# Taking the pairs of a gather and scatter loop two at a time

## The chip, the cores and the metric

The kernel runs on one core of a Trainium2 chip. A core has five engines with queues of their own: TensorE (PE, with its weight loads as PEld), VectorE (DVE), ScalarE (ACT), GpSimd (POOL) and SyncE (SP, which here only issues DMAs). The metric is the time of one execution on the device in microseconds, the median of several runs. A profile is one more execution, recorded by the hardware profiler.

## The reference

All is float32. `x` has 12,500 rows of 256. `src`, `dst` and `edge_weight` describe 200,000 edges, sorted by `dst`.

```python
# graph part
z   = layernorm(x)
s   = z @ W
x   = x + segment_sum(s[src] * edge_weight[:, None], dst) + b
# feed-forward part: the mean over all rows picks 2 of 8 experts for all rows
z   = layernorm(x)
w   = routing(mean(z) @ Wr + br)              # softmaxes, top 2, their weights
y_e = gelu(z @ W1[e] + b1[e]) @ W2[e] + b2[e]
x   = x + layernorm(sum_e w_e * y_e + z) * gamma + beta
```

The kernel moves the product with `W` behind the sum: it sums the weighted rows of `z` by `dst` first and multiplies the sums by `W`.

## The kernel before, in words

**Layout.** `acc` (in SBUF) holds the sums of all nodes, transposed: 128 features on the partitions, two halves, one column a node. `xn` (in DRAM) holds the normalised rows. Edges are taken from the highest `dst` down in chunks of 128; four chunks are a super, two supers (8 chunks, 1,024 edges) are a *pair*. There are 180 pairs; the 128 chunks with the lowest `dst`, where edges are dense, are left to the dense path below.

**A pair** has these steps. `gather_pair` (line 480): GpSimd issues eight indirect DMAs (line 486), each of which fetches 128 rows of `xn` into the tile `g`. `select` (437): VectorE builds, for each chunk, a 128x32 matrix with an edge's weight in the column of its node (line 448; in the early pairs lines 462 and 468), and for each super a 128x128 matrix that shifts the four 32-node windows to their places (lines 456 or 472). `multiply` (494), the first sum: TensorE multiplies each chunk's gathered rows by its selection into 32 partitions of the bank `pt` (line 507); a tiny product ahead of it (502) takes the wait for all eight gathers; ACT copies `pt` to `part` (510). `spread_out` (515), the second level: TensorE multiplies `part` by the shifts into the bank `ps` (522), and VectorE adds it to `acc` (541) at a column read from the data. `g` and the selections have three buffers each, `part` two, `pt` and `ps` one bank each.

**The loop over pairs** (898) writes an order by hand, and each engine runs its own instructions in that order: multiply pair i; select and gather pair i+1; spread out pair i-1; the dense steps; jobs; stages. So a gather may start when the multiply of the pair three before has released its buffer.

**Dense path** (`dense_steps`, 683). In the first 44 pairs VectorE builds 128 chunks' one-hot factors (606, 609), TensorE multiplies them (620) and VectorE adds the products to a count matrix kept in a free part of `acc` (634). Then the matrix is multiplied with all rows of `xn` (662), placed, and its room cleared (677). `prepare_dense` (557) makes the keys, from an iota on GpSimd (561), in tiles of its own.

**Stages.** When all edges of a block of 256 nodes are in, four stages follow, one an iteration: `product` (722) multiplies by `W` (730), adds the row and the bias (726, 731) and takes statistics on VectorE; `normalised` (741); `transposed` (754, line 759; the last bias is added at 768); `keep` stores the block's `zT` to DRAM and `enqueue` (879) makes its jobs known. There are 49 blocks. After 24 and after 38 blocks `name_slot` guesses an expert from the mean so far and loads its weights.

**Jobs.** A job is a block under one guessed expert, 98 in all: four first-level steps (`first`, 822, then GELU on ACT, 823) and two second-level ones (`second`, 830, in the one bank `po`, then VectorE's sums, 836). `work(budget)` runs steps as far as a budget goes: PAIR_US - OWN_US - SLACK_US = 6.5 a pair, less 1.9 and 1.3 where stages run. Steps that are left run in the tail, which mixes the experts' outputs by the true weights, normalises them and stores (lines 1022 to 1074). If a guess was wrong or an edge fell outside its window, a slow path recomputes all; with these inputs it isn't taken.

**Banks.** All eight PSUM banks are in use: `bias_ps` (both biases, broadcast once and read from there by lines 726 and 768), `gz`, `ph` twice, `po`, `pt`, `ps`, `dps`.

Of the kernel before, what the change touches and what calls it, by code (L numbers as in the profile page):

```python
# [18 lines left out]
P = 128  # L19
# [88 lines left out]
def gnn_ffn_kernel(  # L108
# [154 lines left out]
    jobs_stack, stack = ExitStack(), ExitStack()  # L263
    with tc.tile_pool(name="rt", bufs=1) as rt, tc.tile_pool(
        name="bias_ps", bufs=1, space=bass.MemoryType.PSUM
    ) as biasp, jobs_stack, stack, tc.manual_schedule():

# [19 lines left out]
        far = rt.tile([P, 2 * NSEG + 2], FP, name="far")  # L287
        apart = rt.tile([1, NSEG], FP, name="apart")

        sumc = rt.tile([P, H, NBLK], FP, name="sumc")  # L290

        bias_ps = biasp.tile([P, 2, D], FP, name="bias_ps")
        with tc.tile_pool(name="once", bufs=1) as once:
            bias_row = once.tile([1, 2, D], FP, name="bias_row")
            nc.scalar.dma_start(bias_row[:, 0], b_gnn[None, :])
            nc.scalar.dma_start(bias_row[:, 1], beta[None, :])
            nc.tensor.matmul(
                bias_ps.rearrange("p k d -> p (k d)"), row, bias_row.rearrange("p k d -> p (k d)"), start=True, stop=True
            )
        edgep = open_pool(name="edges", bufs=2)  # L300
# [13 lines left out]
        def prepare_segment(k):  # L314
# [50 lines left out]
            nc.vector.scalar_tensor_tensor(gap, gap, float(WIN - NARROW), gap, op0=ALU.subtract, op1=ALU.mult)  # L365
            nc.vector.reduce_max(apart[:, k : k + 1], gap, axis=AX.X)
            t.update(base_i=base_i, rel=rel, slot=slot)

# [46 lines left out]

        gp = open_pool(name="gat", bufs=3)
        selp = open_pool(name="sel", bufs=3)
        partp = open_pool(name="part", bufs=2)
        xp = open_pool(name="xrows", bufs=2)
        pps, aps, dps = psum("part_ps", 1), psum("agg_ps", 1), psum("dense_ps", 1)  # L420
        dp = open_pool(name="dense", bufs=1)

# [10 lines left out]
        selections = {}  # L433
        first_load = -(-DENSE_CHUNKS // DENSE_STEP) + 2
        dense_pairs = first_load + -(-(-(-NQ // 4)) // ROWS_STEP) + 1

# [113 lines left out]
        lots = [(c, LOW) for c in range(0, LOW_END, LOW)] + [(c, HIGH) for c in range(LOW_END, DENSE_CHUNKS, HIGH)]  # L550
        wide = dp.tile([P, QW], FP, name="wide")
        place_of = dp.tile([P, DENSE_CHUNKS], FP, name="place_of")
        key = dp.tile([P, DENSE_CHUNKS], FP, name="key")
        dense_w = dp.tile([P, DENSE_CHUNKS], FP, name="dense_w")
        lot_i = dp.tile([1, len(lots)], I32, name="lot_i")

        def prepare_dense():
            C = DENSE_CHUNKS
            with tc.tile_pool(name="dense_once", bufs=1) as op:
                wide_i = op.tile([P, QW], I32, name="wide_i")  # L560
                nc.gpsimd.iota(wide_i, pattern=[[1, QW]], base=0, channel_multiplier=0)
                nc.vector.tensor_copy(wide, wide_i)
                src_i = op.tile([P, C], I32, name="src_d")
                nc.sync.dma_start(src_i, src[:, :C])
                dst_i = op.tile([P, C], I32, name="dst_d")
                nc.sync.dma_start(dst_i, dst[:, :C])
                nc.sync.dma_start(dense_w, edge_weight[:, :C])
                t_i = op.tile([P, C], I32, name="t_i")
                rel = op.tile([P, C], FP, name="rel_d")
                nc.vector.tensor_scalar(t_i, src_i, P - 1, None, ALU.bitwise_and)  # L570
                nc.vector.tensor_copy(place_of, t_i)
                nc.vector.tensor_scalar(src_i, src_i, 7, None, ALU.logical_shift_right)
                nc.vector.tensor_copy(key, src_i)
                nc.vector.tensor_copy(rel, dst_i)

                base = op.tile([1, C], FP, name="base_d")
                for c0, c1, k in ((0, LOW_END, LOW), (LOW_END, C, HIGH)):
                    n = (c1 - c0) // k
                    nc.vector.tensor_scalar(
                        base[:, c0:c1].rearrange("p (g k) -> p g k", k=k),  # L580
                        rel[0:1, c0:c1].rearrange("p (g k) -> p g k", k=k)[:, :, 0:1].to_broadcast([1, n, k]),
                        0.0,
                        float(DENSE - DENSE_WIN),
                        ALU.max,
                        ALU.min,
                    )
                    g0 = c0 // LOW
                    nc.vector.tensor_copy(
                        lot_i[:, g0 : g0 + n], base[:, c0:c1].rearrange("p (g k) -> p g k", k=k)[:, :, 0]
                    )  # L590
                bcast = scratch_ps()[:, :C]
                nc.tensor.matmul(bcast, row, base, start=True, stop=True)
                nc.vector.tensor_tensor(rel, rel, bcast, ALU.subtract)
                nc.vector.scalar_tensor_tensor(key, key, float(DENSE_WIN), rel, op0=ALU.mult, op1=ALU.add)

                nc.vector.scalar_tensor_tensor(rel, rel, DENSE_WIN - 1.0, rel, op0=ALU.subtract, op1=ALU.mult)
                nc.vector.memset(far[:, 2 * NSEG : 2 * NSEG + 1], -1.0)
                nc.vector.reduce_max(far[:, 2 * NSEG + 1 : 2 * NSEG + 2], rel, axis=AX.X)

# [122 lines left out]
        def product(b):  # L722

            t0 = b * TPB
            xt = rows_of.pop(b)
            nc.vector.tensor_tensor(xt, xt, bias_ps[:, 0].unsqueeze(1).to_broadcast([P, TPB, D]), ALU.add)
            ps = gps.tile([P, TPB, D], FP, name="gz")
# [26 lines left out]
        def transposed(b, z):  # L754

            ps = gps.tile([P, H, TB], FP, name="gz")
            for j in range(TPB):
                for h in range(H):
                    nc.tensor.transpose(ps[:, h, j * P : (j + 1) * P], z[:, j, h * P : (h + 1) * P], ident)
            zT = tp.tile([P, H, TB], FP, name="zT")  # L760
            m = min(TB, N - b * TB)
            for h in range(H):
                nc.scalar.activation(zT[:, h, :m], ps[:, h, :m], AF.Copy, accum_out=sumc[:, h, b : b + 1])
                if m < TB:
                    nc.scalar.activation(zT[:, h, m:], ps[:, h, m:], AF.Copy)
            at = nodes(b * TPB, TPB)
            last_bias = halves(bias_ps[:, 1]).unsqueeze(1).to_broadcast([P, TPB, H, P])
            nc.vector.tensor_tensor(at, at, last_bias, ALU.add)
            return zT
# [124 lines left out]
        stage_z = stage_t = stage_k = None  # L894
        select(0)
        before = None
        g = gather_pair(0)
        for i, (s0, n) in enumerate(pairs):
            k, at = seg_of(s0)
            since = 0 if at + n == segs[k][1] else since + 1  # L900
            if k + 1 < NSEG:
                if since == 0 and k > 0:
                    load_segment(k + 1)
                if since == 4:
                    prepare_segment(k + 1)
            part = multiply(i, g)
            if i + 1 < len(pairs):
                select(i + 1)
                g = gather_pair(i + 1)
            if before:  # L910
                spread_out(*before)
            dense_steps(i)
            before = (i, part)
            complete = nxt > 0 and i > 0 and pairs[i - 1][0] <= done_at[nxt]
            budget = min(budget, 0.0) + PAIR_US - OWN_US - SLACK_US
            budget -= 1.9 * complete + 1.3 * (stage_t is not None)
            if i + 1 < len(pairs):
                budget = work(budget)
            if stage_k is not None:
# [6 lines left out]
            if stage_z is not None:  # L926
                stage_t = (stage_z[0], normalised(*stage_z))
                stage_z = None
            if complete:
                stage_z = (nxt, product(nxt))  # L930
                if nxt >= 2:
                    load_rows(nxt - 2)
                nxt -= 1
        spread_out(*before)
        assert nxt == 0 and stage_z is None and stage_t is None and stage_k is None and named == SLOTS
# [5 lines left out]
        vs = open_pool(name="tail_s", bufs=6)  # L941
        mps = psum("mix_ps", 3)
        gam = tailp.tile([P, D], FP, name="gam")
# [65 lines left out]
        def banks():  # L1009
# [4 lines left out]
            while True:  # L1014
                yield from (m, z, m, lambda: bias_ps, m) if jobs_left() else (m, h, z, m, h, lambda: bias_ps, m, o)

# [316 lines left out]
```

## Time and profile before

| | |
|---|---|
| median of 3 runs | 2438.74 us (2431.86 to 2442.75) |
| the profiled execution | 2448.85 us, of which the span of instructions is 2446.9 us |
| TensorE busy | 1718.6 us (70%) |
| GpSimd busy | 1488.0 us (61%), of it gathers 1368.3 us, 1,436 of 953 ns |
| VectorE busy | 1190.5 us (49%) |
| ACT busy | 475.8 us (19%) |
| DMA | 349.17 MB, mean 143 GB/s |
| mean granted TensorE clock | 0.876 |
| first gather starts, last copy of a first sum starts | 87.56 us, 2265.4 us into the span |

A profile's line names the source line, the engine, the operation and the tiles by the program's names, output first. In rows in order of time the first two numbers are start and length in us; what is in brackets is how long the engine had been idle and what, by the semaphores, ended the wait ("issue": nothing that the profile shows; "remote": a source it can't name). Ends of matmuls are modelled by the profiler, not observed.

### The profile page before, as it was taken

What the parts mean: (1) busy time and instruction counts of PE and PEld (TensorE: products, weight loads), DVE (VectorE), ACT (ScalarE), POOL (GpSimd) and SP (SyncE); (2) the same over time, 40 slices, a digit from 0 to 9 for tenths busy, and PEclk for the clock granted to TensorE, in tenths of its full rate; (3) what the DMA queues carried; (4) which work ended last, traced back from release to release, by engine and by line L of the source; (5) the groups of instructions that cost most, each with busy time, mean ns of one, the idle gap of its engine ahead of it and who ended that gap; (6) DMA issues with size and microseconds to landing.
All of it is one profiled execution on the core that took longest, in us unless ns stands there. A gap on an engine that the chain in (4) does not pass through costs nothing.

```text
span 2446.9 us, 29786 instructions
## 1 busy us (share of the span) xinstructions
PE 1718.6 (70%) x9698; PEld 1215.8 (50%) x9698; DVE 1190.5 (49%) x4265; ACT 475.8 (19%) x1085; POOL 1488.0 (61%) x1537
## 2 busy tenths in 40 slices
PE   0056655666567468888888878888887888888775
PEld 0033333333344246656656656566565665565675
DVE  7355555655533544545444444434433433343688
ACT  5201101111101122212122112212121211211233
POOL 5666656665565666666666666666666666665144
PEclk9987767877788779999999989999998999989898
DMA  8533333332375344444444454444444444444486
GB/s 304 193 91 116 103 93 102 109 114 83 116 225 167 110 145 142 136 138 139 141 131 135 138 151 144 133 134 141 133 136 125 137 137 134 130 123 120 160 281 219
DMA packets 167602, 349.17 MB, mean 143 GB/s; under 512 B 33514, under 2 KB 77072, under 8 KB 167440
## 3 DMA queue, kind: packets, MB, share of 16 engines
q0 software_dynamic: 68928, 188.31, 27.2%
q1 hardware_dynamic: 94120, 145.65, 17.6%
q10 hardware_dynamic: 4392, 13.21, 1.4%
q8 instruction: 82, 1.34, 0.2%
q14 instruction: 80, 0.66, 0.1%
HBM read 282.91 MB, written 64.14 MB: 142 GB/s over the span
## 4 chain that ended last, share of the span: by engine, by line
PE 48%; another core or an unknown queue 17%; DVE 16%; issue 12%; ACT 4%; DMA 2%; POOL 1%; SPq 0%; ACTq 0%; DVEq 0%; POOLq 0%
PE ph L822 14%; PE po L830 12%; PE ps L522 5%; PE pt L507 5%; PE dps L620 4%; PE gz L730 3%; DVE st L69 2%; PE dps L662 2%; DVE acc L541 1%; ACT hT L823 1%; ACT xt L393 1%; ACT part L510 1%; DVE nmt L1052 1%; DVE w L609 1%
## 5 line engine op out<-in xcount | busy, mean ns | idle before, releaser
L486 POOL DMA_INDIRECT g<-xn,src_i x1436 | 1368.3, 953 | 810.4 <-issue 394.2
L822 PE MATMUL ph<-zTj,w 128*128 128x256 f32 x1568 | 452.0, 420 | 127.5 <-issue 55.0
L830 PE MATMUL po<-hT,w 128*128 128x256 f32 x1568 | 438.3, 412 | 105.9 <-issue 80.9
L541 DVE TENSOR_TENSOR acc<-acc,ps 128x256 f32 x359 | 151.0, 421 | 678.8 <-remote 293.2
L822 PEld LDWEIGHTS ph<-zTj,w 128*128 128x128 f32 x1568 | 309.9, 208 | 229.0 <-issue 101.7
L830 PEld LDWEIGHTS po<-hT,w 128*128 128x128 f32 x1568 | 314.8, 206 | 197.6 <-issue 125.7
L510 ACT ACTIVATE part<-pt 128x512 f32<-128x512 f32 (+1 forms) x180 | 107.2, 596 | 1145.2 <-remote 596.2
L620 PE MATMUL dps<-w 128*128 128x490 f32 x256 | 151.5, 718 | 146.3 <-DVE acc L634 113.7
L823 ACT ACTIVATE hT<-ph,b 128x256 f32<-128x256 f32 x392 | 178.6, 472 | 311.2 <-PE ph L822 173.2
L448 DVE TENSOR_SCALAR sel<-iota,rel,wgt 128x32 f32<-128x32 f32 x992 | 233.4, 319 | 0.0
L522 PEld LDWEIGHTS ps<-spread,part 128*128 128x128 f32 x1436 | 186.8, 203 | 93.6 <-issue 87.0
L522 PE MATMUL ps<-spread,part 128*128 128x128 f32 x1436 | 223.3, 301 | 11.4 <-DVE acc L541 8.8
L507 PE MATMUL pt<-g,sel 128*32 128x256 f32 x2872 | 219.9, 418 | 0.0
L836 DVE SCALAR_TENSOR_TENSOR yT<-po,b,zTj 128x256 f32<-128x256 f32 x196 | 85.7, 479 | 163.1 <-PE po L830 73.5
L730 PE MATMUL gz<-wg,acc 128*128 128x256 f32 x392 | 120.0, 460 | 49.0 <-remote 15.2
L620 PEld LDWEIGHTS dps<-w 128*128 128x128 f32 x256 | 52.5, 232 | 203.6 <-DVE acc L634 133.8
L502 PE MATMUL pt<-g,sel 128*32 128x8 f32 (+1 forms) x360 | 42.4, 190 | 131.3 <-DMA g<-xn,src_i 71.6
L502 PEld LDWEIGHTS pt<-g,sel 128*32 128x32 f32 x360 | 26.2, 113 | 204.1 <-issue 165.2
L730 PEld LDWEIGHTS gz<-wg,acc 128*128 128x128 f32 x392 | 89.3, 233 | 74.3 <-issue 37.1
L731 DVE TENSOR_TENSOR acc<-gz,xt 128x512 f32<-128x512 f32 x49 | 33.9, 691 | 167.7 <-PE gz L730 107.1
L507 PEld LDWEIGHTS pt<-g,sel 128*32 128x32 f32 x2872 | 98.7, 118 | 26.2 <-issue 8.8
L1044 POOL TENSOR_TENSOR rst<-vet,half 128x4 f32<-128x4 f32 (+1 forms) x25 | 42.4, 1697 | 108.4 <-DVE vet L1042 108.4
(183 smaller groups left out, 1586.6 us busy)
## 6 DMA issues: line engine op xcount, KB each, us to landing
zTj<-zts SPq DMA_DIRECT2D x98, 256.0 KB
yts<-yT SPq DMA_DIRECT2D x98, 256.0 KB
ab<-yts SPq DMA_DIRECT2D x48, 512.0 KB
g<-xn,src_i POOLq DMA_INDIRECT x1436
zts<-zT SPq DMA_DIRECT2D x49, 256.0 KB
xt<-in_x SPq DMA_DIRECT2D x24, 512.0 KB
xn<-xt ACTq DMA_DIRECT2D x24, 512.0 KB
xt<-in_x SPq DMA_DIRECT2D x48, 256.0 KB
```

Of the source, the lines that this page charges most:

```text
L448: nc.vector.tensor_scalar(sel[:, j * SUPER + c], iota[:, :NARROW], t["rel"][:, col], t["wgt"][:, col], ALU.is_equal, ALU.mult,)
L486: nc.gpsimd.indirect_dma_start(out=g[:, j], out_offset=None, in_=xn, in_offset=bass.IndirectOffsetOnAxis(ap=segment[k]["src_i"][:, col : c ...
L507: nc.tensor.matmul(pt[q, j // SUPER], sel[:, j], g[:, j], start=True, stop=True, tile_position=(0, j % SUPER * NARROW))
L510: nc.scalar.activation(part[:, :n], pt[:, :n], AF.Copy)
L522: nc.tensor.matmul(ps[:, j, h], part[:, j, h * P : (h + 1) * P], spread[:, j], start=True, stop=True)
L541: nc.vector.tensor_tensor(at, at, ps[:, j], ALU.add)
L620: nc.tensor.matmul(ps, r, q, start=(c == c0), stop=(c == c0 + k - 1))
L730: nc.tensor.matmul(ps[:, j], node_tile(t0 + j)[:, h], wg[:, h], start=(h == 0), stop=(h == H - 1))
L822: nc.tensor.matmul(ph, w1[:, k, h, c * P : (c + 1) * P], zT[:, h], start=(h == 0), stop=(h == H - 1))
L823: nc.scalar.activation(hT[:, c], ph, AF.Gelu, bias=b1[:, k, c : c + 1])
L830: nc.tensor.matmul(po[:, h], w2[:, k, c, h * P : (h + 1) * P], hT[:, c], start=(c == 0), stop=(c == FC - 1))
L836: nc.vector.scalar_tensor_tensor(yT[:, i], po[:, i], b2[:, k, i : i + 1], zT[:, i], op0=ALU.add, op1=ALU.add)
```

## The change

The loop takes two pairs an iteration, and `g` and the selections get four buffers. Within an iteration the order is now: segment preparation; gather both pairs of the next iteration; a quarter of the jobs; spread out the first pair of the iteration before and its dense steps; a quarter of the jobs; the second pair likewise; select both pairs of the next iteration; the stages with the third quarter; the product of a completed block and the last quarter; then multiply both pairs of this iteration, into two `pt` banks. The budget is twice the old one, and a block's stages advance once an iteration.

The second `pt` bank is `bias_ps`'s: the biases are broadcast through a `ph` bank at the start, copied to SBUF, and read there. The tail's own rotation of banks gets a fourth `mix` bank in its place. The tiles of the dense preparation move into buffers of the job tiles (`hT`, `zTj`), which are not yet in use then. A check is added to the segment preparation (`low_chunk`): that a pair spread while the dense matrix still stands in `acc` doesn't reach into it.

```diff
-    with tc.tile_pool(name="rt", bufs=1) as rt, tc.tile_pool(
-        name="bias_ps", bufs=1, space=bass.MemoryType.PSUM
-    ) as biasp, jobs_stack, stack, tc.manual_schedule():
+    with tc.tile_pool(name="rt", bufs=1) as rt, jobs_stack, stack, tc.manual_schedule():
...
-        apart = rt.tile([1, NSEG], FP, name="apart")
+        apart = rt.tile([1, 2 * NSEG], FP, name="apart")
...
+        low_chunk = SUPER * pairs[dense_pairs + 3][0]
...
-        bias_ps = biasp.tile([P, 2, D], FP, name="bias_ps")
+        bias = rt.tile([P, 2, D], FP, name="bias")
...
+            bias_ps = scratch_ps()
+            nc.tensor.matmul(bias_ps, row, bias_row.rearrange("p k d -> p (k d)"), start=True, stop=True)
+            nc.scalar.activation(bias.rearrange("p k d -> p (k d)"), bias_ps, AF.Copy)
...
+            lo, hi = max(0, low_chunk - s0 * SUPER), min(m, pad)
+            if lo < hi:
+                nc.vector.tensor_scalar(gap[:, lo:hi], base[:, lo:hi], -1.0, float(QH * DENSE), ALU.mult, ALU.add)
+                nc.vector.reduce_max(apart[:, NSEG + k : NSEG + k + 1], gap[:, lo:hi], axis=AX.X)
+            else:
+                nc.vector.memset(apart[:, NSEG + k : NSEG + k + 1], -1.0)
...
-        gp = open_pool(name="gat", bufs=3)
-        selp = open_pool(name="sel", bufs=3)
+        gp = open_pool(name="gat", bufs=4)
+        selp = open_pool(name="sel", bufs=4)
...
-        pps, aps, dps = psum("part_ps", 1), psum("agg_ps", 1), psum("dense_ps", 1)
+        pps, aps, dps = psum("part_ps", 2), psum("agg_ps", 1), psum("dense_ps", 1)
...
+        held = hp.tile([P, FC, TB], FP, name="hT").rearrange("p c t -> p (c t)")
+        wide = held[:, :QW]
...
-            nc.vector.tensor_tensor(xt, xt, bias_ps[:, 0].unsqueeze(1).to_broadcast([P, TPB, D]), ALU.add)
+            nc.vector.tensor_tensor(xt, xt, bias[:, 0].unsqueeze(1).to_broadcast([P, TPB, D]), ALU.add)
...
-        select(0)
-        before = None
-        g = gather_pair(0)
-        for i, (s0, n) in enumerate(pairs):
...
-            part = multiply(i, g)
-            if i + 1 < len(pairs):
-                select(i + 1)
-                g = gather_pair(i + 1)
-            if before:
-                spread_out(*before)
-            dense_steps(i)
-            before = (i, part)
+        def gather_two(i):
+            return [gather_pair(p) for p in range(i, min(i + 2, len(pairs)))]
+
+        for p in range(min(2, len(pairs))):
+            select(p)
+        before = []
+        g = gather_two(0)
+        for i in range(0, len(pairs), 2):
+            two = range(i, min(i + 2, len(pairs)))
+            for p in two:
...
+            ahead = gather_two(i + 2)
             complete = nxt > 0 and i > 0 and pairs[i - 1][0] <= done_at[nxt]
-            budget = min(budget, 0.0) + PAIR_US - OWN_US - SLACK_US
+            budget = min(budget, 0.0) + 2 * (PAIR_US - OWN_US - SLACK_US)
             budget -= 1.9 * complete + 1.3 * (stage_t is not None)
-            if i + 1 < len(pairs):
-                budget = work(budget)
+            part_of = budget / 4
+
+            def some(share):
+
+                nonlocal budget
+                if i + 2 < len(pairs):
+                    budget = share * part_of + work(budget - share * part_of)
+
+            some(3)
+            for b, p in zip(before, two):
+                spread_out(*b)
+                dense_steps(p)
+                some(2)
+            if not before:
+                for p in two:
+                    dense_steps(p)
+            for p in range(i + 2, min(i + 4, len(pairs))):
+                select(p)
             if stage_k is not None:
...
+            some(1)
             if complete:
...
+            some(0)
+            before = [(p, multiply(p, t)) for p, t in zip(two, g)]
+            g = ahead
+        for b in before:
+            spread_out(*b)
...
-        mps = psum("mix_ps", 3)
+        mps = psum("mix_ps", 4)
...
-                yield from (m, z, m, lambda: bias_ps, m) if jobs_left() else (m, h, z, m, h, lambda: bias_ps, m, o)
+                yield from (m, z, m, m, m) if jobs_left() else (m, h, z, m, h, m, m, o)
```

## The prediction

> **What bounds the kernel now.** I read the stages first, then GpSimd's waits, then one pair in order of time. The stages, in microseconds from the span's start (each engine's busy time, then its instructions):
>
> ```profile
> core 0: us, PE busy (x) PEld busy (x) DVE busy (x) ACT busy (x) POOL busy (x), PEclk, DMA share, GB/s
> 174.00:680.00 506.00, 301.07 (x1496) 165.21 (x1496) 291.47 (x932) 58.89 (x152) 310.54 (x320) 0.77 0.36 107
> 680.00:787.00 107.00, 78.37 (x432) 54.97 (x432) 32.15 (x112) 10.84 (x27) 60.92 (x64) 0.86 0.62 194
> 880.00:2260.00 1380.00, 1136.88 (x6409) 834.08 (x6410) 582.39 (x2288) 281.29 (x652) 878.12 (x928) 0.92 0.46 137
> 2260.00:2447.00 187.00, 129.13 (x932) 118.25 (x930) 145.29 (x376) 57.93 (x120) 70.19 (x37) 0.87 0.64 217
> ```
>
> In the long stage 880 to 2260 TensorE is busy 82% and GpSimd 64%, so TensorE looks like the bound. GpSimd's own waits between 900 and 2200 say otherwise (total, times, longest):
>
> ```profile
> POOL g L486 <- issue: 233.0, 763, 0.6
> POOL g L486 <- remote: 132.5, 62, 2.3
> POOL g L486 <- PE ph L822: 76.7, 36, 2.3
> POOL g L486 <- PE po L830: 19.1, 9, 2.2
> ```
>
> 763 waits of 0.30 us lie between two gathers of a pair; some 107 waits (62 + 36 + 9) are all about 2.1 us, one a pair. A late TensorE would leave waits of all lengths. In order of time (start, length, engine; lines left out):
>
> ```profile
> 1401.95 0.60 ACT L510 ACTIVATE part<-pt 128x512 f32<-128x512 f32 x1 [3.25 <-PE po L830]
> 1402.13 0.94 POOL L486 DMA_INDIRECT g<-xn,src_i  x1 [2.16 <-PE po L830]
> ...
> 1407.44 1.03 PE L507 MATMUL pt<-g,sel 128*32 128x256 f32 x13
> ...
> 1408.40 1.16 PE L522 MATMUL ps<-spread,part 128*128 128x128 f32 x8
> ...
> 1410.87 0.95 POOL L486 DMA_INDIRECT g<-xn,src_i  x1 [0.30 <-issue]
> ...
> 1413.81 0.60 ACT L510 ACTIVATE part<-pt 128x512 f32<-128x512 f32 x1 [10.29 <-remote]
> ...
> 1413.99 0.96 POOL L486 DMA_INDIRECT g<-xn,src_i  x1 [2.17 <-remote]
> ...
> 1414.83 1.99 PE L822 MATMUL ph<-zTj,w 128*128 128x256 f32 x8 [0.72 <-ACT hT L823]
> ```
>
> The multiply (L507) starts at 1407.4 and its record ends at 1408.47, but the copy that needs only it (L510) starts at 1413.81, and GpSimd, which needs the multiply's buffer for its next pair, at 1413.99. The last gather had ended at 1411.82. I took this distance for every pair: in 106 of the 115 pairs from number 62 to 176 the copy starts 1.8 to 2.15 us after the last gather's end (median 1.94), while the multiply's record ended a median 6.1 us before the copy. So a multiply issued while gathers run **counts as done only when the gathers have drained**. The loop is closed: eight gathers of 1.25 us less the last 0.30 (9.7), 1.95 of draining, 0.17 of restart = 11.8 us; measured 11.90 a pair there. Whatever follows the multiply is held too: with the semaphore updates in the trace matched to the records, first-level steps (L822) behind a multiply in a burst complete a median 2.92 us after their recorded end (172 of them), those with no multiply ahead of them 0.17 (138).
>
> **Two pairs an iteration.** Call R the release, when both multiplies count as done. GpSimd then gathers 16 without a stop: 16 x 1.25 - 0.30 = 19.7; restart 0.2, draining 1.95: **21.85 us for two pairs** against 2 x 11.90 = 23.8, if TensorE has issued both multiplies by then. Two pauses of 2.1 become one. With four buffers GpSimd never waits inside the 16: the first needs the first multiply, the ninth the second, released together.
>
> Is TensorE there in time? Its passes between 892 and 2211, at their full-clock distance (0.2155 us for 256 columns, 0.11 for 128), make 8.14 us a pair, so 16.3 for two, 14.2 of it ahead of the multiplies (about 1.03 each). At the clock of 0.92 that is 15.5. After a release TensorE resumes 0.7 to 1.9 us late (above 0.72, on ACT's gelu); I take 1.5, with two copies of 0.60 now ahead on ACT. I add 1 for waits on DVE and ACT: R + 18. Then VectorE: selections of both pairs come together, 2 x (8 x 0.319 + 2 x 0.28) = 6.2 us in one piece, and behind them on its queue wait the second level's sums (L836), for which the one po bank and so the next L830 waits. Two first-level steps (1.7) cover part; up to 4 us could be bare, I take 2 in half of the iterations: R + 18 to R + 20, released at the drain or, when just late, some 2 us after. So **22.4**, bounds 21.85 and 23.5.
>
> [...] A multiply is 18 passes with 18 loads; two make 72. [...]
>
> [...]
>
> **The dense stages.** In 174 to 680 a pair takes 12.7 us; TensorE has 5.3 of full-clock work, at 0.77: 13.8 for two. The chain in an iteration: copy 0.8, first spread 1.2, three dense products 3.2 (0.82 each, clock in), the lot's sum 0.9, second spread 1.2, VectorE makes and three products again 4.2, transposes and product 2.8: R + 14.3 to R + 17 with multiplies, under 19.9. Every eighth iteration also prepares a segment in front (L320 to L366, about 5 us). **22.5**. In 680 to 787 the rows' products (24 passes, 6.9 us a pair) make two pairs 15.7/0.86 = 18.3 plus waits: 23.5. Pairs 54 to 63 have little for TensorE: 22.0.
>
> **Start.** Pairs 0 to 3 are gathered in one run (28 gathers, 87.6 to 122.5). The iota of the dense preparation now stands behind 28 gathers on GpSimd's queue instead of 12. It used to run at 102.5; at 122.5, VectorE's cast, the preparation behind it, TensorE's broadcast and both first multiplies wait for it. They can't release their buffers before the drain at 124.5 in any case: R for pairs 0 and 1 is 127.5. The old restart there was 126.7.
>
> **Small edits.** Bias from SBUF: 98 sums of 0.679; by L1068 (128x1024 from SBUF, 1.274, half of it 0.64) 0.64 to 0.68 each, 0 to -4 us of VectorE, hidden since it is busy 42%. The extra check: two small operations in some of 12 segments (L323's 0.21 and L366's 0.27), at most 6 us, same cover; bare they would cost those 6. One more ACT copy at setup, under 1. Gathers, loads and stores keep their number; SP's queue keeps the order of its loads and stores, with those of two pairs together, and the three loads of the dense preparation stay ahead of the first steps. The stage steps advance once in two pairs: by the loop's conditions slots are named at pairs 64 and 112 instead of 61 and 108, and six first and five second steps more stay for the tail (14 and 9 against 8 and 4): 6 x 0.86 + 5 x 1.72 = 13.8 us of TensorE, which has 58 idle there; I take +3 (0 to 14). The tail's banks stay as many.
>
> **The sum.** Start 127.5. Releases of pairs 2 to 177 are 88: 22 x 22.5 + 4 x 23.5 + 5 x 22.0 + 57 x 22.4 = 1976. Loading weights at two namings 5. The last pairs' spreads and multiplies 7.5 (now 2260.4 to 2267). Tail 180 + 3. Together 2299, against the span of 2446.9: 148 less. The profiled execution took 2448.85, span and 2 around it, 10 over the median of 2438.74; the same 10 off 2301 gives **2290**.
>
> **Rivals.** (a) The floor: TensorE is always in time, every step 21.85: 88 x 21.85 = 1923 and 323 for the rest, 2246 span, **2238**. For it: 4.6 us of TensorE's idle a pair are in the hold. (b) TensorE or VectorE often late, still faster: 23.3 a step, **2365**. For it: VectorE's 6.2 us block. (c) No change in the pace: the hold is TensorE's own lateness, or the job steps lose elsewhere what the pause gives: **2440**. Against it: the equal distances. (d) Slower: the multiplies stand last in the order, so every delay of TensorE's queue, above all L830 waiting for L836 behind the selections, goes straight into GpSimd's pause. It decides from a mean step of 24.1 ((2446.9 - 323)/88), which is issue at R + 22; at 25, **2515**. For it: nothing gathers ahead beyond two pairs. Against it: between release and multiply TensorE runs gapless after its resumption, with the clock's share as work.
>
> **Numbers.** Likeliest 0.58 (its own range 2250 to 2345), floor 0.11, (b) 0.16, (c) 0.04, (d) 0.11. The first three are faster: 0.85; same 0.04, slower 0.11. 0.5% is what a measurement here can tell from no change. The range takes in the floor and most of (b): 2230 to 2385.
>
> **What would show it.** GpSimd's pauses half as many, each about 2.1 to 2.7 us, bursts of 16; the copies L510 in couples 1.95 us after a burst's last gather; first-level steps soon done inside a burst; GpSimd busy about 68% in the job stage (16 x 0.95 in 22.4). Wrong would be: pauses over 4 us as a rule (TensorE late; look for L830 <- L836), or steps without a multiply ahead held as well.

## The result, and the profile after

The changed kernel took **2891.2 us** (median of 4 runs, 2879.1 to 2898.0) against 2440.7 before on the same chip (2431.9 to 2449.1): a ratio of **1.187, 95% interval 1.181 to 1.193**. The forecast was 2290, range 2230 to 2385, and faster. Time and sign are both wrong.

The stages of the changed kernel (us from the span's start; then busy time of TensorE, its weight loads, VectorE, ACT and GpSimd with their instructions, granted TensorE clock, DMA share, GB/s). The job stage lies now between the gathers of pairs 62 and 176, 909 to 2629:

```profile
174.00:680.00 506.00, 307.06 (x1446) 172.80 (x1445) 286.37 (x918) 54.33 (x142) 296.42 (x308) 0.77 0.34 100
680.00:787.00 107.00, 62.59 (x336) 44.65 (x336) 24.97 (x80) 7.83 (x22) 56.81 (x60) 0.78 0.59 182
909.00:2629.00 1720.00, 1116.14 (x6203) 868.37 (x6202) 570.63 (x2262) 284.06 (x638) 867.55 (x913) 0.79 0.36 108
2673.00:2896.00 223.00, 151.69 (x1052) 138.56 (x1052) 147.86 (x394) 63.05 (x131) 69.03 (x37) 0.84 0.55 188
```

In the job stage neither engine is busy: TensorE fell from 82% to 65% and GpSimd from 64% to 50%, where 68% was forecast. GpSimd's waits and the two largest others in that stage (total, times, longest):

```profile
POOL g L491 <- PE pt L512: 583.1, 54, 21.3
DVE acc L546 <- remote: 436.0, 48, 16.6
ACT hT L827 <- PE ph L826: 362.1, 182, 18.3
POOL g L491 <- issue: 252.8, 829, 0.6
```

As forecast there is one pause of GpSimd in two pairs (57 in that stage), but it lasts 591.5 / 57 = 10.4 us on the mean, not 2.1 to 2.7, and it waits for the multiplies (L512). Two pairs take 1719.5 / 57 = 30.2 us. The second row tells more: VectorE waits 9 us at a time for the spreads (L527), which have no multiply ahead of them in a burst (a run of gathers without a pause). One iteration of the changed kernel in order of time (lines left out):

```profile
1621.49 0.94 POOL L491 DMA_INDIRECT g<-xn,src_i  x1 [7.87 <-PE pt L512]
...
1626.69 10.92 SPq L844 DMA_DIRECT2D yts<-yT  x2
1626.72 3.72 PE L834 MATMUL po<-hT,w 128*128 128x256 f32 x16
...
1628.55 0.88 DVE L546 TENSOR_TENSOR acc<-acc,ps 128x256 f32 x2 [1.89 <-remote]
...
1630.28 1.05 PE L527 MATMUL ps<-spread,part 128*128 128x128 f32 x8
...
1636.38 0.88 DVE L840 SCALAR_TENSOR_TENSOR yT<-po,b,zTj 128x256 f32<-128x256 f32 x2 [6.95 <-remote]
...
1640.22 0.95 POOL L491 DMA_INDIRECT g<-xn,src_i  x1 [0.30 <-issue]
...
1640.78 0.32 SPq L820 DMA_DIRECT2D zTj<-zts  x1
...
1643.44 6.20 PE L826 MATMUL ph<-zTj,w 128*128 128x256 f32 x16 [12.11 <-DMA zTj<-zts]
1644.12 0.88 DVE L546 TENSOR_TENSOR acc<-acc,ps 128x256 f32 x2 [6.86 <-remote]
...
1651.37 1.03 PE L512 MATMUL pt<-g,sel 128*32 128x256 f32 x13
1652.55 0.60 ACT L515 ACTIVATE part<-pt 128x512 f32<-128x512 f32 x1 [2.41 <-PE pt L512]
1652.73 0.95 POOL L491 DMA_INDIRECT g<-xn,src_i  x1 [11.56 <-PE pt L512]
```

The second-level step (L834) ends by its record at 1630.44, and VectorE's sums that need only it (L840) start at 1636.38. The second spread (L527) ends at 1631.33, and its sum (L546) starts at 1644.12, 2.95 us after the burst's last gather ended at 1641.17. TensorE does nothing from 1631.3 to 1643.4: it waits for a block's `zTj`, whose load stands on SyncE's queue behind the store of what the late L840 writes (L844) and is issued at 1640.78. (Such a wait for `zTj` is rare: three in that stage, 36.4 us. TensorE's larger one is for the gelus, L827: 156.2 us in 28 waits.) After the drain, when what was held comes through, TensorE has 8 us of work left ahead of the multiplies, and GpSimd waits for it.

### The profile page after: what moved, and what is told of

It is laid out like the page before. It is cut to its first block, busy times and chain, and to the rows that moved or that the text cites. A ratio compares the mean times of both kernels' runs of the same rounds, so it can differ in the third digit from the quotient of the medians.

```text
span 2895.9 us, 29781 instructions
## 1 busy us (share of the span) xinstructions
PE 1759.3 (61%) x9698; PEld 1306.9 (45%) x9698; DVE 1189.9 (41%) x4281; ACT 483.4 (17%) x1086; POOL 1491.4 (52%) x1537
## 4 chain that ended last, share of the span: by engine, by line
PE 35%; another core or an unknown queue 34%; DVE 12%; issue 11%; ACT 3%; DMA 3%; SPq 1%; POOL 1%; DVEq 0%; ACTq 0%; POOLq 0%
PE ph L826 10%; PE po L834 8%; PE pt L512 5%; PE gz L734 5%; PE ps L527 3%; DVE acc L546 2%; DVE sel L453 1%; PE dps L624 1%; DVE st L69 1%; PE dps L666 1%; DVE yT L840 1%; ACT xt L401 1%; ACT zT L767 1%; DMA ab<-yts 1%
## 5 line engine op out<-in xcount | busy, mean ns | idle before, releaser
L826 PE MATMUL ph<-zTj,w 128*128 128x256 f32 x1568 | 453.7, 432 | 250.2 <-ACT hT L827 156.2
L546 DVE TENSOR_TENSOR acc<-acc,ps 128x256 f32 x359 | 151.2, 421 | 859.2 <-remote 537.6
L834 PE MATMUL po<-hT,w 128*128 128x256 f32 x1568 | 422.6, 418 | 97.8 <-DVE yT L840 78.5
L826 PEld LDWEIGHTS ph<-zTj,w 128*128 128x128 f32 x1568 | 324.4, 217 | 336.8 <-ACT hT L827 170.1
L834 PEld LDWEIGHTS po<-hT,w 128*128 128x128 f32 x1568 | 325.7, 212 | 168.0 <-DVE yT L840 88.4
L734 PE MATMUL gz<-wg,acc 128*128 128x256 f32 x392 | 167.8, 602 | 310.0 <-ACT zT L767 179.6
L827 ACT ACTIVATE hT<-ph,b 128x256 f32<-128x256 f32 x392 | 180.4, 472 | 893.3 <-PE ph L826 410.7
L527 PE MATMUL ps<-spread,part 128*128 128x128 f32 x1436 | 225.1, 307 | 103.9 <-DVE acc L546 44.9
L527 PEld LDWEIGHTS ps<-spread,part 128*128 128x128 f32 x1436 | 209.9, 216 | 151.9 <-issue 82.2
L734 PEld LDWEIGHTS gz<-wg,acc 128*128 128x128 f32 x392 | 114.6, 305 | 350.2 <-ACT zT L767 187.0
L512 PE MATMUL pt<-g,sel 128*32 128x256 f32 x2872 | 228.1, 424 | 41.2 <-issue 40.9
L840 DVE SCALAR_TENSOR_TENSOR yT<-po,b,zTj 128x256 f32<-128x256 f32 x196 | 85.8, 479 | 389.3 <-PE po L834 157.4
L767 ACT ACTIVATE zT<-gz 128x256 f32<-128x256 f32 (+1 forms) x98 | 36.6, 379 | 684.4 <-remote 518.5
L512 PEld LDWEIGHTS pt<-g,sel 128*32 128x32 f32 x2872 | 102.3, 119 | 83.4 <-issue 63.3
L666 PE MATMUL dps<-w,acc 128*96 128x256 f32 x196 | 58.5, 468 | 49.4 <-DVE acc L546 32.3
```

Source lines behind the costliest of these rows:

```text
L512: nc.tensor.matmul(pt[q, j // SUPER], sel[:, j], g[:, j], start=True, stop=True, tile_position=(0, j % SUPER * NARROW))
L527: nc.tensor.matmul(ps[:, j, h], part[:, j, h * P : (h + 1) * P], spread[:, j], start=True, stop=True)
L546: nc.vector.tensor_tensor(at, at, ps[:, j], ALU.add)
L734: nc.tensor.matmul(ps[:, j], node_tile(t0 + j)[:, h], wg[:, h], start=(h == 0), stop=(h == H - 1))
L826: nc.tensor.matmul(ph, w1[:, k, h, c * P : (c + 1) * P], zT[:, h], start=(h == 0), stop=(h == H - 1))
L827: nc.scalar.activation(hT[:, c], ph, AF.Gelu, bias=b1[:, k, c : c + 1])
```

## The experiments

(The edits of the runs are shown shortened.) Two theories at first. **H**: TensorE's completions, of more than multiplies, are held while GpSimd's gathers run without a pause. **O**: the order, with its chains over VectorE and ACT and the multiplies last, makes TensorE late whatever the gathers do.

The runs of one comparison share a chip, and on two of our chips, as on that of the profiles above, the kernel before took 2440 to 2454 us, while on four others it took 2086 to 2089; so every ratio is to the kernel before on the same chip, and I call the first sort *holding* chips, for what their traces show.

**Gathers replaced by plain loads**, on a holding chip, in the order after and in the order before. The sums are of wrong rows, so the guessed experts are wrong and the program runs on into its slow path; only the stretch up to that is read.

```diff
-                nc.gpsimd.indirect_dma_start(out=g[:, j], ..., in_=xn, in_offset=...)
+                r0 = (s0 * SUPER + j) % (N // P) * P
+                nc.sync.dma_start(g[:, j], xn[r0 : r0 + P])
```

> The changed kernel with GpSimd's gathers replaced by ordinary loads of 128 consecutive rows each, issued on SyncE's queue: the same bytes in the same place of the order, but of other rows, so the sums are of wrong rows. Theory H (TensorE's completions are held while GpSimd's gathers run without a pause): the spreads and transposes complete within some 0.3 us of their recorded end, the gap between the second spread and the next TensorE work (12 us in the iteration at 1620) goes, two pairs take 18 to 20 us (16.3 us of TensorE's work at a clock near 0.9), and the time falls to 2000 to 2200. Theory O (the order with the multiplies last, and the chain of TensorE, VectorE and ScalarE in it, makes TensorE late whatever the gathers do): two pairs stay at 28 us or more, 2650 or more. A third, C (the memory traffic itself holds TensorE): lags of several us stay, with the time at 2600 or more.

> The kernel before with the same replacement (gathers become loads of 128 consecutive rows each on SyncE's queue, wrong rows). Theory H: the copy of a multiply follows its recorded end by under 0.5 us instead of 6.1, a pair takes 9 to 10 us, bound by TensorE, and the time is 2000 to 2250. Theories O and C: 11.9 us a pair stay, about 2400.

The 900 to 1700 stretch, first of the changed kernel so altered:

```profile
900.00:1700.00 800.00, 740.01 (x4841) 612.20 (x4839) 424.75 (x1682) 221.25 (x485) 0.00 (x0) 0.96 0.57 176
```

and of the kernel before so altered, with one multiply of it in order of time and the copy that needs it:

```profile
900.00:1700.00 800.00, 760.12 (x4942) 615.77 (x4940) 428.33 (x1698) 226.87 (x492) 0.00 (x0) 0.99 0.58 180
```

```profile
1409.03 1.03 PE L501 MATMUL pt<-g,sel 128*32 128x256 f32 x13
...
1410.15 0.60 ACT L504 ACTIVATE part<-pt 128x512 f32<-128x512 f32 x1 [2.35 <-PE pt L501]
```

TensorE is busy 92% and 95%; the copy follows the multiply's end at 1410.06 by 0.09 us, and in both traces the median completion comes 0.01 to 0.1 us after the recorded end for every kind of operation. From pair 62 to 176 a pair takes 9.33 us in the order after and 9.04 in the order before, and the last stores are issued at 1957 and 1917. More bytes a second flowed than with gathers (176 and 180 GB/s against 108 and 137), so the amount of traffic doesn't do it. H stands; O falls: the order costs 3% here, not 19.

**A wait between the two pairs' gathers**, holding chip.

```diff
-            ahead = gather_two(i + 2)
+            ahead = [gather_pair(i + 2)]
...
                 spread_out(*b)
+                if p == two[-1]:
+                    nc.vector.tensor_copy(token[:, 0:1], ps[0:1, 0, 0, 0:1])
+                    nc.gpsimd.tensor_copy(token[:, 1:2], token[:, 0:1])
+                    ahead.append(gather_pair(i + 3))
```

> The changed kernel, its order on TensorE untouched, with one wait more: the second pair's eight gathers start only when VectorE has added up the second spread of the iteration (one small copy on VectorE and one on GpSimd). Theory H: the wait breaks the burst of 16 into two of 8 with a drain between them, at which the held work comes through, so added waiting makes it faster: two pauses of 2 to 4 us and 19.4 of gathers, 24 to 27 us for two pairs, 2430 to 2650. Theory O: TensorE is as late as before and GpSimd later by up to 10 us: 31 us for two pairs or more, 2890 to 3300.

2795.2 us, 1.137 (1.130 to 1.144) of before. A wait of GpSimd more in each iteration, and it is nearer to the kernel before than the change is (1.187): the sign that H gives. The size missed 2430 to 2650, for two reasons. The wait often only moved the pause: of 78 bursts in the job stage 32 are still of 16 gathers, an iteration's second pair and the next one's first. And the added wait itself is long:

```profile
POOL token L908 <- DVE token L907: 375.4, 53, 13.6
```

Seven microseconds at a time, for the second spread. All pauses of GpSimd in that stage make 515 us, against 591.5 after the change.

**The other parts alone**, holding chip: the loop of before, with four buffers, two `pt` banks, the bias in SBUF and the tables in job tiles.

> The other parts of the change alone: one pair at a time in the order of before (multiply, selection, gather, spread, dense, work), but with four buffers, two banks for the sums, the bias in SBUF and the dense tables in two tiles. Theory H: a multiply still waits for the drain of a burst of eight, so the pace is that of before, 2400 to 2460. Theory O says the same. A theory P (one of these other parts costs the time, for instance a bank or buffer shared anew): 2600 or more.

2489.9 us, 1.014 (1.010 to 1.018). The pace from pair 62 to 176 is 12.17 us against 11.87. I had costed these edits at nothing; together they cost 1.4% here, a small part of 18.7. Which of them, was not taken apart.

**Everything short at the end.** Here I supposed (H2) that only what stands at or behind a pass of few columns is held; H1 is that all is, from some 6 us into a burst on.

```diff
-                spread_out(*b)
...
-                stage_k = (stage_t[0], transposed(*stage_t))
...
             some(0)
+            for b in before:
+                spread_out(*b)
...
+                stage_k = (stage_t[0], transposed(*stage_t))
...
+                select(p)
             before = [(p, multiply(p, t)) for p, t in zip(two, g)]
```

> The changed kernel with everything short on TensorE moved to the end of an iteration: the jobs and the dense products first, then the aggregation's product, then both spreads, the transposes and the two multiplies one after the other (the selections stand behind the spreads). Burst of 16, buffers and number of operations are as in the change. Theory H2 (in a burst only what comes at or behind a short pass is held: multiplies, 128-column spreads and transposes; 256-column passes with none of them ahead are not): the jobs complete within 0.3 us inside the burst, the short passes are issued near its end, two pairs take 22 to 25 us, 2250 to 2500. Theory H1 (all of TensorE's completions are held from some 6 us into a burst on, whatever stands ahead): jobs lag by 5 to 12 us, 28 us or more for two pairs, 2700 or more. Theory O: 2850 to 2950, as the same chains are there.

> As the kernel with everything short at the end, but only the two spreads are moved; the transposes stay ahead of the product, in the middle of the burst, in the iterations that have them (24 of some 58 in the job stage). Theory H2: iterations without transposes take 22 to 25 us, those with them 28 to 31, in all 2350 to 2650. H1 and O: 2700 or more.

> The kernel with everything short on TensorE at the end of an iteration, once more. Where the kernel before takes about 2087, a ratio of 1.037 again. Where it takes about 2440: theory H2 (only what stands at or behind a short pass in a burst is held) 2250 to 2500; theory H1 (all is held from some 6 us into a burst on) 2700 or more.

> The kernel with everything short on TensorE at the end of an iteration, wanted on a chip that holds completions, which shows by the time of the kernel before, about 2440. There theory H2 (only what stands at or behind a short pass in a burst is held) says 2250 to 2500, theory H1 (all is held from some 6 us into a burst on) 2700 or more. On a chip where the kernel before takes about 2087 it says nothing new: a ratio of 1.035.

The first three fell on chips without holding: 1.037 (1.034 to 1.040), 1.043 (1.041 to 1.045) and 1.033 (1.031 to 1.036), which tell H1 from H2 in nothing. The fourth fell on a holding chip: 2917.5 us, 1.192 (1.183 to 1.200). H2 falls. The jobs, wide passes with nothing short ahead of them, are now late themselves:

```profile
POOL g L491 <- PE pt L512: 613.8, 51, 20.2
ACT hT L827 <- remote: 555.7, 92, 13.9
```

**TensorE's order of before, bursts of 16.** On the version with the other parts alone, with buffers that each hold two pairs:

```diff
-        gp = open_pool(name="gat", bufs=4)
+        gp = open_pool(name="gat", bufs=2)
...
-                g = gather_pair(i + 1)
+            if i % 2 == 0:
+                gs.update({p: gather_pair(p) for p in (i + 2, i + 3)})
```

> TensorE's order of before (one pair at a time: multiply, selection, spread, dense, work), with the change's other parts, but two pairs share one buffer of double size, of which there are two, so GpSimd gathers 16 without a stop as in the change. Theories H1 and H2 (the burst's length costs the time): the multiply at the start is followed by its spread and the work behind it, all held for most of 20 us: 28 to 34 us for two pairs, 2700 to 3100. Theory O (the order does it): 22 to 25 us, 2250 to 2500.

> The kernel with TensorE's order of before and bursts of 16, once more. Where the kernel before takes about 2087, a ratio of 1.015 again. Where it takes about 2440: theories H1 and H2 (the length of the burst costs the time) 2700 to 3100; theory O (the order does it) 2250 to 2500.

> The kernel with TensorE's order of before and bursts of 16, wanted where the kernel before takes about 2440. There the length of the burst as the cause (H1, H2) says 2700 to 3100, the order as the cause (O) 2250 to 2500. Where the kernel before takes about 2087: a ratio of 1.013 again.

Without holding 1.0145 (1.013 to 1.016) and 1.0115 (1.010 to 1.013). On a holding chip 2977.4 us, **1.216 (1.211 to 1.222)**, two pairs in 30.3 us, with the same waits as after the change:

```profile
POOL g L495 <- PE pt L516: 603.9, 56, 21.6
ACT part L519 <- remote: 538.2, 39, 19.8
```

So where completions are held the length of the burst costs the time, with either order.

**The changed kernel again**, on a chip without holding:

> The changed kernel as it is, once more. The kernel before took 2440 to 2454 in some of our comparisons and 2086 to 2088 in others, which ran on other chips, and in the traces of the latter every TensorE operation completes within 0.15 us of its recorded end though the gathers run. Theory H (the held completions are the whole loss): where the kernel before takes about 2087, the changed kernel has no lags and takes 2090 to 2180, a ratio of 1.00 to 1.045; where it takes about 2440, the ratio is 1.18 again. Theory O (the order makes TensorE late whatever the gathers do): a ratio of 1.15 or more on either.

2129.9 us, **1.0205 (1.0185 to 1.0225)**. GpSimd's waits from 900 to 1900, and one iteration in order of time:

```profile
POOL g L491 <- issue: 229.3, 753, 0.3
POOL g L491 <- PE pt L512: 6.5, 3, 5.9
```

```profile
1407.12 0.94 POOL L491 DMA_INDIRECT g<-xn,src_i  x1 [0.30 <-issue]
1407.15 1.03 PE L512 MATMUL pt<-g,sel 128*32 128x256 f32 x13
...
1408.33 0.60 ACT L515 ACTIVATE part<-pt 128x512 f32<-128x512 f32 x1 [0.33 <-PE pt L512]
...
1411.67 1.05 PE L527 MATMUL ps<-spread,part 128*128 128x128 f32 x8
...
1412.82 0.88 DVE L546 TENSOR_TENSOR acc<-acc,ps 128x256 f32 x2 [5.69 <-issue]
```

The copy follows the multiply in the middle of running gathers, the sum follows its spread by 0.1 us, and the longest lag of 658 operations is 0.12 us. GpSimd pauses three times in the whole kernel. The new order with its two selections in a block and its multiplies last is in time at a pace of 10.2 us a pair. It is 2% slower all the same: there was no drain to save, and from pair 62 to 176 it loses 20 us, of which 8 in two pauses and 912 x 0.0137 = 12 in gathers of 0.961 instead of 0.947 us; the tail takes 206 us after the last gather instead of 188. (The trace that stands for the kernel before is the one with halved passes, which took the same time there.)

**Gathers as plain loads on GpSimd's own queue.** Wrong rows again.

```diff
-                nc.gpsimd.indirect_dma_start(out=g[:, j], ..., in_=xn, in_offset=...)
+                nc.gpsimd.dma_start(g[:, j], xn[r0 : r0 + P])
```

> The changed kernel with the indirect gathers replaced by plain loads of 128 consecutive rows each, still issued by GpSimd on its own queue: same bytes, wrong rows, so the program runs on into its slow branch and only the stretch up to there is read. If every load that GpSimd issues from its own queue holds TensorE (theory S): lags of 5 us and more for the short passes, some 28 us for two pairs. If only the indirect gathers do (theory I): lags under 0.3 us, 18 to 21 us for two pairs.

No lag, 9.43 us a pair; but the chip was one without holding, so nothing is told apart.

**First-level passes halved in width**, in the kernel before.

```diff
+            for t in range(0, TB, P):
                 for h in range(H):
-                    nc.tensor.matmul(ph, w1[...], zT[:, h], ...)
+                    nc.tensor.matmul(ph[:, t : t + P], w1[...], zT[:, h, t : t + P], ...)
```

> The kernel before with the first level's passes halved in width: each product of 256 columns made as two of 128, the same result. Theory H2 (short passes are what is held): a first-level step with no multiply ahead of it in the burst, which completes 0.17 us after its recorded end in the kernel before, now lags by 2 us or more, and so does what follows it; the time grows to 2550 to 2900. Theory H1 (time since the burst's start) and theory M (the multiplies' narrow tiles or their gathered operand are what is held): lag under 0.5 us, and only TensorE's own time grows, by up to 0.2 us a step: 2440 to 2520.

> The kernel before with the first level's passes halved in width (128 columns instead of 256), wanted where the kernel before takes about 2440. There theory H2 (short passes are what is held) says that first-level steps with no multiply ahead of them in a burst lag by 2 us or more instead of 0.17, and 2500 to 2900 in all; theory M (only the multiplies, spreads and transposes, for what they read) says lags under 0.5 us and 2440 to 2520. Where the kernel before takes about 2087: no change.

Without holding 1.001 (1.000 to 1.002). On a holding chip 2497.9 us, 1.020 (1.014 to 1.027), and of the first-level steps with no multiply, spread or transpose ahead of them in the burst a quarter now lags by over 4.2 us (196 steps, by the start of the gelu that needs them), where it was a quarter over 0.57 (194). TensorE's busy time for the same work hardly grew (1078 us in 900 to 2200, 1075 before); there are only more passes.

That and the lags of seven kernels on holding chips (before, after, the pause, the parts, short at the end, bursts of 16, halved passes) give a measure that none of the theories had: the **number of TensorE passes since the burst's first gather**. I matched semaphore updates to records, in order, in the job stage and call an operation held if it completes over 0.3 us after its recorded end. Share held (operations), 3,113 in all, of those that end 2 us or more ahead of the burst's end:

```
us since the     passes since the burst's start
burst's start    0-15         16-23        24-31        32 and over
0 to 4           0.16 (851)   0.37 (192)   0.84 (43)    1.00 (9)
4 to 6           0.06 (36)    0.29 (177)   0.67 (245)   0.97 (275)
6 and over       0.17 (12)    0.50 (30)    0.95 (60)    0.99 (1178)
```

Read across, the share goes from a sixth or less to all; read down, it changes less and not always the same way, so H1 falls too. Behind fewer than 16 passes little is held, at 16 to 23 a third to a half, from 32 on nearly all.

The matching is in part inferred: these traces have about a tenth fewer updates than operations that make one (1,079 for 1,188 in the kernel before, 1,061 for 1,184 after the change). The gelus need no matching, for each follows one first-level step. Of 1,435 steps in the seven kernels for whose result ScalarE had waited, the gelu starts over 0.6 us after the step's recorded end in 12% of those behind 0 to 15 passes, 23% at 16 to 23, 63% at 24 to 31 and 97% from 32 on; with the loads on SyncE's queue, on a holding chip, in none of 561.

**Fewer passes**, the test of that count: the jobs' products left out whole (the diff; the sums then read a job's input), and in part (one of two kept at the first level, one of four at the second).

```diff
         def first(k, zT, hT, c):
+            return
...
-            for c in range(FC):
-                nc.tensor.matmul(po[:, h], w2[...], hT[:, c], ...)
...
-                        yT[:, i], po[:, i], b2[...], zT[:, i], ...
+                        yT[:, i], zT[:, i], b2[...], zT[:, i], ...
```

> The changed kernel with the jobs' products and gelu left out (VectorE writes each job's result from its input; loads, stores and all else stay). Theory N (counted over seven kernels that show held completions: from 24 to 32 TensorE passes after the start of a burst of gathers on, nothing completes until the gathers pause, whatever the passes are and with little regard to time): 16 to 28 passes are left ahead of the multiplies instead of some 75, so nothing TensorE waits for is held, both multiplies are issued inside the burst, and the prediction's own step of 22 us for two pairs comes about in the job stage, with GpSimd's pauses near 2.1 us; on a chip where the kernel before takes about 2440 that is some 2896 - 57 x 8 less a shorter tail, 2350 to 2450. If what stays (selections on VectorE, the order) is late by itself: 26 us or more for two pairs, 2600 or more. Where the kernel before takes about 2087, the gathers set the pace and it is 2050 to 2120.

> The kernel before with the jobs' products and gelu left out in the same way. Theory N: the burst of eight and its drain stay the bound, 11.85 us a pair (23.7 for two) in the job stage, so where the kernel before takes about 2440 it still takes 2380 to 2440, and against it the changed kernel without jobs has the gain that was predicted in that stage, some 1.7 us for two pairs. Where the kernel before takes about 2087: 2030 to 2090.

> The changed kernel with part of the jobs' products left out: one of two at the first level, one of four at the second, so a job is 12 passes instead of 32; gelu, sums, loads and stores stay. Theory N: some 40 to 50 passes are left ahead of the multiplies, over the 24 to 32 that complete in a burst, so some of the work and both multiplies come behind the drain: 24 to 28 us for two pairs in the job stage, 2500 to 2700 where the kernel before takes about 2440. Where it takes about 2087: 2090 to 2140.

They fell on a chip without holding: 2110.7, 2090.9 and 2113.2 us, 1.0105, 1.0011 and 1.0117. That the count alone makes the prediction's step fail is therefore not tested: it is a pattern over kernels, the halved passes among them. Nor does any run part a count of passes from one of the weight loads that go with them. What they do show is what bounds both kernels on such a chip. The 900 to 1900 stretch of the changed kernel, with its jobs (the run above) and without:

```profile
900.00:1900.00 1000.00, 866.58 (x5430) 703.66 (x5428) 487.02 (x1910) 249.52 (x546) 754.66 (x787) 0.93 0.53 158
900.00:1900.00 1000.00, 428.56 (x2804) 280.54 (x2796) 475.11 (x1880) 95.55 (x216) 761.39 (x784) 0.59 0.53 157
```

Half of TensorE's work is gone and GpSimd's pace is the same (784 gathers, 787 with the jobs): 1.25 us a gather sets the time.

## Why the prediction was wrong, step by step

- **"GpSimd is in a closed loop, and a multiply issued while gathers run counts as done only when they have drained."** Right for the kernel before on holding chips, and shown: with plain loads on SyncE's queue the lag is gone (a median 0.01 to 0.1 us). Not a property of every chip: on one without holding the longest of 658 lags is 0.12 us.
- **"Whatever follows the multiply is held too", those with none ahead are not.** This is the step that failed. It read as a property of the multiply what goes, in these traces, with the number of passes. In the kernel before a multiply's record ends some 35 passes after the burst's start, 18 of them its own: it was itself what took the count from some 17 to there, and the steps without a multiply ahead were simply the early ones. The trace of before had it: by the matching above its held share is 0.21, 0.35 and 0.68 for the first three groups of eight passes, and 0.98 for the next. I split the lags by the kind of work ahead and not by its amount.
- **"R + 18 to R + 20".** The term that went wrong with it. On the second chip, where nothing is held, an iteration's multiplies start a mean 16.6 us after the end of the last ones and take 2.1, about R + 19; on the holding chip they start after 27.8, about R + 30. There an iteration has 73 passes ahead of its multiplies, most of them chained over ACT or VectorE, and little completes in a burst behind some 30 passes (by the table 0.67 to 0.95 are held at 24 to 31, 0.97 to 1.00 from 32 on). The kernel before has two bursts in two pairs, and so some 30 twice; the change has one, and the rest waits for the pause. Between the drain and the next gather a mean of 45 passes starts in the changed kernel, multiplies included; 1 in the kernel before.
- **"22.4" a step.** Measured 30.2; 57 steps make 443 of the 597 us between the span and the 2299 forecast. **Dense stages, 22.5**: from pair 4 to 62 26.7 on the mean, some 119 us over the forecast; GpSimd waits 168.6 us for the multiplies there, and what makes these late in that stage was not taken apart. **Start, 127.5**: 2 over. **Tail, +3 (0 to 14)**: it takes 223.7 us after the last gather against 188.3, and the end from pair 176 on is 33 over the forecast; together that is the 597. Of the longer tail 18 us show on the other chip too, more than the 14 that I bounded the left-over steps with; with the jobs' products left out the two tails there differ by 1 us (184.9 and 183.6), so it is the jobs.
- **VectorE's double selection and L830 behind L836**, the named danger: on the chip without holding GpSimd waits for the multiplies three times, 6.5 us, from 900 to 1900. Rival (d) had the right place (multiplies last, so every delay goes into GpSimd's pause), but not the mechanism, and at 2515 its size was far too small. Both signs that I gave for wrong came: pauses over 4 us, and "steps without a multiply ahead held as well".
- **Rival (a), "4.6 us of TensorE's idle a pair are in the hold".** A wrong reading. By its records TensorE is idle 2.1 us a pair in all (busy 82% of 11.9), and 1.5 us of it lies between a multiply's recorded end and its copy; 4.6 was the work that it does there.
- **Rival (c), "the hold is TensorE's own lateness".** Not so: on a holding chip, in either order, TensorE's operations complete a median 0.01 to 0.1 us after their recorded ends once the gathers are loads on SyncE's queue, though it is busy 92% and 95%. By what way GpSimd's gathers make them late there, no run shows.
- **Small edits at nothing.** 1.4% together on a holding chip.

## What to carry to other kernels

Before lengthening a run of DMAs that GpSimd issues, tabulate how late TensorE's completions come by the number of passes since the run began, not by what the passes are; a pause that looks like waste may be where the other engine's work gets through, as here on a holding chip a mean of 45 passes an iteration. Time a change of this sort on more than one chip: here the same change cost 19% on one kind and 2% on the other. Where GpSimd's gathers set the pace, at 1.25 us each on the chips without holding, regrouping the work around them gained nothing (a ratio of 1.0205).

## What the runs showed of the hardware that I had not expected

- The kernel before took 2440 to 2454 us on some chips and 2086 to 2089 on others, though a gather takes 0.946 us with 0.30 between two on both. Nor do the gathers' packets differ: from 900 to 1700 they take 155 ns on the mean on either sort (25,872 of them in the kernel before, 30,701 in the one with halved passes). The difference that shows is in when TensorE's operations count as done during gathers. Whether it belongs to the chip or to what else went on there, and by what way it comes about, is open.
- On holding chips the share held is 0.06 to 0.17 behind fewer than 16 passes since GpSimd's gathers began, and 0.97 to 1.00 from 32 on; during 16 gathers in a row results of TensorE came 5.9 and 12.8 us late in the iteration shown. With loads on SyncE's queue at 176 to 180 GB/s none of 561 gelus starts over 0.6 us after its step's recorded end. These loads differ from the gathers in the engine that issues them, in having no indices and in reading rows that lie together; which of these matters is open, for loads that GpSimd issues without indices were not tried on such a chip.
